# Four graph layers on one core: node batches started inside the edge sums, and window sums added into SBUF by VectorE

## The chip, the cores and the metric

The kernel runs on one core of one Trainium2 chip. The metric is the device time of that core in microseconds, the median of the runs of a kernel. The kernel before took 8477.11 us (median of 3 runs, 8463.03 to 8496.4). Its profile is one more execution, which took 6808.89 us; every duration taken from the profile belongs to that execution.

Names of engines: PE is TensorE, DVE is VectorE, ACT is ScalarE, POOL is GpSimd, SP is the engine that issues most DMAs.

## The reference

6,250 nodes with 128 features and 100,000 edges sorted by target node go through four layers. Each layer is added to its input and normalized by row.

```python
x = _layernorm(x + L0(x, edges))                 # two attention convolutions
x = _layernorm(x + L1(x, edges, edge_weight))    # weighted graph convolution
x = _layernorm(x + L2(x, node_vec, edges, ...))  # relational attention, 8 heads
x = _layernorm(x + L3(x, edges))                 # messages summed by target, then a gated unit

# L0, for each of its two convolutions (edges and self loops):
g = h @ W; e = leaky_relu(s[src] + d[dst]); m = segment_max(e, dst)
ex = exp(e - m[dst]); z = segment_sum(ex, dst)
out = segment_sum(g[src] * (ex / z[dst])[:, None], dst) + bias
# L1: out[dst] += (x @ W)[src] * dis[src] * w * dis[dst];   L3: agg[dst] += (h @ W_msg)[src]
# L2: softmax by target of q[dst] . k(message), times v(message); message from x[src] and the relation
```

The targets are drawn as 6250 times the square of a uniform number, so low node numbers have many more edges than high ones.

## The kernel before, in words

**Blocks and steps.** Nodes lie in NB = 49 blocks of 128. Edges are brought into K = 832 steps; a step holds at most 128 edges, all of one block of targets, and blocks come in rising order. `SRCT` holds the source node of each edge, `DLT` its place in the block, `OFF` the window offsets of the steps. The layout is made at the start (lines 134 to 289), where a flag (`unsorted`, lines 181 to 188) branches past a sort that this input doesn't need.

**Edge stages.** Five stages sum over all steps: `attention_edges` twice (lines 434 to 533), `sum_edges` for the convolution (line 681, weighted by the edge) and for the last layer (line 1010), and the value sum of layer 2 (lines 940 to 958). In the first four, each step begins with one gather of 128 rows from a table in HBM, an indirect DMA that POOL issues (`gather`, lines 132 to 134). A matrix of zeros and ones, `sel`, with the step's edges as rows and the 128 places of the block as columns, is then multiplied by the gathered rows on PE, which adds the edges up by target.

**The sums (`Windows`, lines 388 to 432).** M = 8 steps share a window of up to 9 blocks, laid out over three PSUM banks, with two such windows in rotation. For each window PE writes zeros into the three banks (line 412), adds eight step products at an offset that it holds in a register (line 415), and adds the old sum of the window's first block with an identity matmul out of SBUF (line 422; with a factor, line 426, at the first window of an attention chunk). ACT then copies the whole window, 1,224 columns, to the accumulator `ACC` in SBUF (line 431). So the next window's line 422 waits for ACT's copy.

**Attention chunks.** `attention_edges` goes in chunks of T = 64 steps: 64 gathers, small matmuls for the target's term (lines 467 and 470), then a chain of scans on DVE and transposes on PE that finds the maximum by target (lines 475 to 522), then the scaling on ACT (line 532) and the sums. In the first pass `row_selections` (lines 373 to 385) makes a bf16 matrix from a row that SP loads to all partitions (`dlrow`, line 381, two pieces per 16 steps, two buffers).

**Node stages.** Between two edge stages lies work by node, for 13 groups of up to 4 blocks (`GROUPS`): merging the sums, transposes, the next layer's matmuls, and the table in HBM that the next edge stage gathers from (lines 625 to 638, 642 to 648, 658 to 680, 683 to 693, 746 to 767, 961 to 977, 998 to 1009). All of it begins after the last edge sum. A whole-row normalization (`stats`, `inverse_root`, `normalize`, lines 322 to 343) first collects the statistics of all 49 blocks, then takes the root, then scales block by block on DVE. The last node stage (lines 1011 to 1046) writes the output in two DMAs.

**The score stage of layer 2 (lines 769 to 871).** It walks all steps in groups of 4: `rows_of` issues 4 gathers from `XAt`, 4 loads of query rows and 2 row loads; `messages` forms the message; `keys` transposes it, copies it out of PSUM on ACT and multiplies by the key and value weights; `scores` follows every 16 steps. In trip n it issues `rows_of(n+1)`, `messages(n)`, `keys(n-1)`. After it, lines 873 to 936 join the maxima of all steps, with no gather.

**What sets the order.** [...] A scheduler in the building layer places the instructions of a region by data dependence and source order, and may move an instruction past others within the region; it doesn't move anything across an `If`.

## Time and profile before

| | us |
|---|---|
| median of the runs | 8477.11 |
| the profiled execution | 6808.89 |
| its span, first to last instruction | 6807.1 |
| POOL busy | 4198.3 |
| PE busy | 4236.0 |
| ACT busy | 2223.4 |
| DVE busy | 1797.6 |
| gathers, four edge stages | 3,328 |
| gathers, score stage | 832 |

The page gives the busy time of each engine, the span in 40 slices, and the groups of equal instructions with the idle time before them. The timeline of one engine lists its instructions with start, length and, in brackets, the idle time before and what ended it. A table by stage gives the busy time of every engine in chosen stretches of the span; the stretches that the prediction shows begin and end at the first and the last gather of a stage. [...]

### The profile page before, as it was taken

How to read it: one execution, taken by the hardware profiler on the slowest of the kernel's cores; microseconds unless marked ns; L12 is line 12 of the kernel's file. 1: busy time of each engine (PE TensorE's matmuls, PEld its weight loads, DVE VectorE, ACT ScalarE, POOL GpSimd, SP SyncE). 2: the span in 40 equal slices, each digit the busy share in tenths (PEclk: the TensorE clock that was granted, in tenths of full speed). 3: DMA queues.
4: the chain of work that ended last, by engine and by line, in shares of the span. 5: the costliest groups of instructions: out<-in, count | busy, mean ns of one | idle time of the engine just before them, and what ended most of it. 6: DMA issues, size and time to landing. Idle time of an engine off the chain costs nothing. (4 is left out here: it accounts for less than half of the span.)

```text
span 6807.1 us, 75064 instructions
## 1 busy us (share of the span) xinstructions
PE 4236.0 (62%) x21755; PEld 2971.6 (44%) x21755; DVE 1797.6 (26%) x4328; ACT 2223.4 (33%) x5686; POOL 4198.3 (62%) x4384
## 2 busy tenths in 40 slices
PE   3355554434454546666656888888867756767676
PEld 2244433333343434444434556555545544444443
DVE  4122222300000040000017777777730030000005
ACT  1243333233333323444434444455412221111112
POOL 1777777277777627777753666666524426777771
PEclk9566666666556665555557989999968875555557
DMA  4455555344444333333336888899746634333331
GB/s 121 142 159 153 160 166 146 106 125 122 129 134 141 107 93 108 103 108 102 109 86 189 238 239 245 245 260 261 228 144 203 207 103 125 103 108 102 109 102 32
DMA packets 736418, 997.90 MB, mean 147 GB/s; under 512 B 151184, under 2 KB 593352, under 8 KB 702744
## 3 DMA queue, kind: packets, MB, share of 16 engines
q1 hardware_dynamic: 587410, 662.03, 30.3%
q0 software_dynamic: 146992, 331.03, 19.3%
q8 instruction: 197, 3.23, 0.2%
q14 instruction: 197, 1.61, 0.1%
q10 hardware_dynamic: 1622, 0.01, 0.0%
HBM read 824.55 MB, written 168.09 MB: 146 GB/s over the span
## 5 line engine op out<-in xcount | busy, mean ns | idle before, releaser
L415 PE MATMUL win<-g,sel 128*128 128x128 f32 (+2 forms) x6656 | 1710.9, 412 | 747.8 <-issue 250.8
L133 POOL DMA_INDIRECT g<-g,SRCT x1664 | 1578.6, 949 | 722.2 <-issue 492.9
L415 PEld LDWEIGHTS win<-g,sel 128*128 128x128 f32 x6656 | 1348.1, 288 | 1246.1 <-issue 457.3
L431 ACT COPY ACC<-win 128x1224 f32 x520 | 610.9, 1175 | 1992.4 <-PE win L422 1745.2
L133 POOL DMA_INDIRECT xa<-xat,SRCT x832 | 823.2, 989 | 538.8 <-issue 319.4
L133 POOL DMA_INDIRECT g<-yt,SRCT x832 | 785.0, 943 | 394.5 <-issue 388.1
L133 POOL DMA_INDIRECT g<-mt,SRCT x832 | 785.1, 944 | 355.0 <-issue 246.8
L412 PE MATMUL win<-zero 1*128 1x512 bf16 x1560 | 618.0, 495 | 32.4 <-ACT ACC L431 27.6
L549 ACT ACTIVATE g<-g,EWT 128x128 f32<-128x128 f32 x832 | 318.5, 399 | 608.8 <-DMA g<-yt,SRCT 607.3
L532 ACT ACTIVATE g<-g 128x128 f32<-128x128 f32 x1664 | 516.5, 390 | 0.0
L835 PE MATMUL pk<-Wkv,mT 128*128 128x256 f32 x1664 | 461.0, 409 | 32.3 <-ACT mT L828 22.7
L952 POOL TENSOR_TENSOR vx<-v,exh 128x512 f32<-128x512 f32 x208 | 217.7, 1062 | 424.4 <-PE win L415 268.2
L422 PE MATMUL win<-ACC,ident 128*128 x982 | 270.8, 371 | 157.9 <-ACT ACC L431 157.8
L415 PE MATMUL win<-vx,sel 128*128 128x136 f32 x1664 | 281.4, 337 | 124.2 <-issue 118.1
L835 PEld LDWEIGHTS pk<-Wkv,mT 128*128 128x128 f32 x1664 | 300.8, 199 | 95.4 <-ACT mT L828 53.8
L840 ACT COPY kv<-pk 128x512 f32<-128x512 f32 x416 | 242.2, 589 | 302.1 <-issue 187.9
L415 PEld LDWEIGHTS win<-vx,sel 128*128 128x128 f32 x1664 | 265.7, 242 | 155.7 <-issue 145.4
L477 DVE TENSOR_TENSOR de<-de,g 128x16 f32<-128x16 f32 x104 | 17.2, 184 | 1093.9 <-DMA g<-g,SRCT 1093.9
L422 PEld LDWEIGHTS win<-ACC,ident 128*128 128x128 f32 x982 | 221.6, 277 | 170.1 <-ACT ACC L431 170.1
L1029 DVE SCALAR_TENSOR_TENSOR n<-pn,bhh,gate 128x512 f32<-128x512 f32 (+1 forms) x13 | 9.4, 720 | 1053.5 <-ACT gate L1021 1053.0
L483 PE MATMUL pch<-ident,e 128*64 128x128 f32 x26 | 10.8, 416 | 443.6 <-DVE e L479 443.6
L814 ACT ACTIVATE z<-rp,TMT 128x128 f32<-128x128 f32 x832 | 238.2, 374 | 145.5 <-DVE msg L811 143.5
(329 smaller groups left out, 4878.0 us busy)
## 6 DMA issues: line engine op xcount, KB each, us to landing
sel<-seld SPq DMA_DIRECT2D x208, 1024.0 KB
qb<-qt SPq DMA_DIRECT2D x832, 102.0 KB
seld<-sel SPq DMA_DIRECT2D x52, 1024.0 KB
vt<-kv SPq DMA_DIRECT2D x208, 256.0 KB
v<-vt SPq DMA_DIRECT2D x208, 256.0 KB
g<-g,SRCT POOLq DMA_INDIRECT x1664
dlrow<-dlr SPq DMA_DIRECT2D x104, 256.0 KB
rseld<-rsel SPq DMA_DIRECT2D x52, 512.0 KB
```

Source lines behind the costliest of these rows:

```text
L133: nc.gpsimd.indirect_dma_start(out=dst_tile, out_offset=None, in_=tab, in_offset=bass.IndirectOffsetOnAxis(ap=idx, axis=0))
L412: nc.tensor.matmul(self.win[:, i, :], zero[:, 0:P], zero, start=True, stop=False, skip_group_check=True)
L415: nc.tensor.matmul(flat_[:, ds(self.at[q], n)], sel, rows, start=False, stop=False, skip_group_check=True)
L422: nc.tensor.matmul(self.win[:, 0, 0:n], ident, ACCF[:, ds(before, n)], start=False, stop=True, skip_group_check=True)
L431: nc.scalar.copy(ACCF[:, ds(self.to[w], (M + 1) * W)].rearrange("p (b w) -> p b w", b=SB), self.win[:, :, 0:SB * W])
L477: nc.vector.tensor_add(de[:, i * U:(i + 1) * U], de[:, i * U:(i + 1) * U], g[:, :, D])
L532: nc.scalar.activation(g[:, q, 0:D], g[:, q, 0:D], AF.Copy, scale=g[:, q, D:D + 1])
L549: nc.scalar.activation(g[:, q, :], g[:, q, :], AF.Copy, scale=EWT[:, k0 + q:k0 + q + 1])
L814: nc.scalar.activation(z[:, q, :], rp[:, q, D:], AF.Copy, scale=TMT[:, k0 + q:k0 + q + 1])
L835: nc.tensor.matmul(pk[:, q - q0, :], mT[:, q, :], Wkv, start=True, stop=True)
L840: nc.scalar.copy(kv[:, q0:q0 + 2, :], pk)
L952: nc.gpsimd.tensor_mul(vx[:, :, 0:D].rearrange("p q (h d) -> p q h d", h=HD), v.rearrange("p q (h d) -> p q h d", h=HD), exh[:, u0:u0 + B, ...
```

## The change

**Node batches ahead.** Each node stage between edge stages becomes a generator (`to_second`, `to_convolution`, `to_queries`, `to_messages`, `to_output`) for one group of 4 blocks, with a `yield` between its parts. While an edge stage runs, `Ahead.tick` is called after each window and advances one batch by one part; batch j starts at step EARLY[j]. Eleven of the 13 groups have such a place. A flag in a register, made from the layout at the start, says whether a block of these groups still had edges at its place; if so, all eleven are done again in an `If` after the stage. The last two groups (5 blocks) follow the `If`, part by part in turn.

**Windows.** A window now spans 3 steps (attention, values) or 4 (the two `sum_edges`) in one PSUM bank, with four banks in a ring. `ACC` is set to zero at the start of the stage; DVE adds the bank to `ACC` at an offset that DVE loads itself. The identity matmul and ACT's copy are gone; the factor of an attention chunk is applied to `ACC` by DVE.

```diff
-M = 8
-SB = 3
-T = 64
+WINDOWS = {3: W, 4: D}
+CHUNKS = [48] * 17 + [16]
+T = max(CHUNKS)
+EARLY = [236, 332, 408, 472, 528, 580, 628, 672, 712, 756, 792]
+NE = len(EARLY)
...
+        for j, k in enumerate(EARLY):
+            nc.vector.tensor_scalar(lates[:, j:j + 1], bkrow[0:1, k:k + 1], (j + 1) * B - 0.5, None, op0=OP.is_lt)
...
+    late = nc.values_load(lati, min_val=0, max_val=NE)
...
+    class Ahead:
+        def tick(self, k):
+            if k - self.last < 4 and k < K:
+                return
+            self.last = k
+            if self.on is None and self.j < NE and k >= EARLY[self.j]:
+                self.on = self.batch(*GROUPS[self.j])
+                self.j += 1
+            if self.on is not None and next(self.on, self) is self:
+                self.on = None
+        def finish(self, again=None):
+            while self.on is not None or self.j < NE:
+                self.tick(K)
+            with tc.If(late > 0):
+                if again is not None:
+                    nc.sync.dma_start(X[:, 0:NE * B, :], again)
+                for j in range(NE):
+                    for _ in self.batch(*GROUPS[j]):
+                        pass
+            rest = [self.batch(*g) for g in GROUPS[NE:]]
+            while rest:
+                rest = [r for r in rest if next(r, self) is not self]
...
+            for t0 in range(0, NB + MW, 14):
+                nc.vector.memset(ACC[:, t0:min(NB + MW, t0 + 14), :], 0.0)
...
+            bank = self.ring[:, k // m % self.banks, :]
+            if k % m == 0:
+                nc.tensor.matmul(bank[:, 0:m * w], zero[:, 0:P], zero[:, 0:m * w], start=True, stop=False,
+                                 skip_group_check=True)
+                self.fade = None
+            nc.tensor.matmul(bank[:, ds(self.at[k % U], n)], sel, rows, start=False, stop=False,
+                             skip_group_check=True)
...
+                if self.fade is not None:
+                    a0 = ACCF[:, ds(to, kept)]
+                    nc.vector.tensor_scalar(a0, a0, self.fade, None, op0=OP.mult)
+                a0 = ACCF[:, ds(to, m * W)].rearrange("p (b w) -> p b w", w=W)[:, :, 0:n]
+                nc.vector.tensor_add(a0, a0, bank[:, 0:m * w].rearrange("p (b w) -> p b w", w=w)[:, :, 0:n])
+                self.ahead.tick(k + 1)
```

**One batch, as an example.** The merge with the own rows is now done by PE with diagonal matrices, and the normalization is per batch (`norms` on DVE with a root by bit shift and three Newton steps, `normalized` on ACT):

```diff
+        def to_convolution(t0, g):
+            cc = merge_factors(node, SD[1], t0, g)
+            own = own_rows(node, Gt[1], t0, g)
+            yield
+            dg = diagonals(node, (cc[:, 0], cc[:, 1]), g, 2)
+            yield
+            px = batch_of(bank())
+            add_rows(px, g, bl1, t0)
+            for q in range(g):
+                nc.tensor.matmul(px[:, q, :], dg[:, q, 0, :], ACC[:, t0 + q, 0:D], start=False, stop=False,
+                                 skip_group_check=True)
+                nc.tensor.matmul(px[:, q, :], dg[:, q, 1, :], own[:, q, :], start=False, stop=q == g - 1,
+                                 skip_group_check=True)
+            r, m = norms(node, px, g)
+            yield
+            x = X[:, t0:t0 + g, :]
+            normalized(x, px, r, m, g)
+            nc.sync.dma_start(nodes(XS[0])[:, t0:t0 + g, :], x)
+            yield
+            xT = transposed(node, batch_of(bank("nb")), x, g, "hT")
+            yield
+            py = batch_of(bank())
+            for q in range(g):
+                nc.tensor.matmul(py[:, q, :], xT[:, q, :], W1l, start=True, stop=True)
+            y = node.tile([P, B, D], F32, name="own")
+            nc.vector.tensor_mul(y[:, :g], py[:, :g], DIS[:, t0:t0 + g, None].to_broadcast([P, g, D]))
+            nc.sync.dma_start(nodes(Yt)[:, t0:t0 + g, :], y[:, :g])
```

**Buffers.** The node work of layers 0 and 1 shares two single PSUM banks, `na` and `nb`, also for the very first node stage, where there were two buffers each for the transposes and the first product. Gather buffers of 16 steps go from 7 to 6 (attention), stay at 8 in the last `sum_edges` and go from 8 to 6 in the other. The row pieces of the first pass are halved and have one buffer:

```diff
-            for h in range(2):
-                n = U * P // 2
-                row = work.tile([P, n], BF16, name="dlrow")
+            for h in range(4):
+                n = U * P // 4
+                row = work.tile([P, n], BF16, name="dlrow", bufs=1)
```

**Score stage.** Gather buffers `xa` go from 4 to 8, query rows `qb` from 3 to 4, `kv` from 2 to 3, row selections of 4 steps to 4, and the transpose gets a trip of its own. The head's key-bias term of the queries comes from a matmul with a small weight matrix made at the start.

```diff
-                for n in range(-1, steps + 1):
+                for n in range(-1, steps + 2):
                     if n + 1 < steps:
-                        got[n + 1] = rows_of((n + 1))
+                        got[n + 1] = rows_of(n + 1)
                     if 0 <= n < steps:
                         msgs[n] = messages(n, got[n][0], got[n][3])
-                    if 0 <= n - 1:
-                        keys(n - 1, msgs.pop(n - 1), *got.pop(n - 1)[1:3])
+                    if 0 <= n - 1 < steps:
+                        turns[n - 1] = turned(msgs.pop(n - 1))
+                    if 0 <= n - 2:
+                        keys(n - 2, turns.pop(n - 2), *got.pop(n - 2)[1:3])
```

**Output.** `to_output` writes each batch to HBM as soon as it is normalized, in place of two DMAs at the end.

## The prediction, as put on record

> **What bounds the kernel now.** I read the 40 slices first, then the table by stage, then POOL's timeline inside a stage, then the groups. In the slices, POOL stands at seven tenths through most of the kernel, with dips:
>
> ```profile
> POOL 1777777277777627777753666666524426777771
> ```
>
> The table by stage cuts the span at the first and last gather of each stage. Rows in order: start, first attention pass, gap, second pass, gap, convolution sums, gap, score stage, gap, value sums, gap, message sums, end. Columns after the stretch: its length, busy time (instructions) of PE, its weight loads, DVE, ACT and POOL, the granted PE clock, the DMA share, GB/s.
>
> ```profile
> core 0: us, PE busy (x) PEld busy (x) DVE busy (x) ACT busy (x) POOL busy (x), PEclk, DMA share, GB/s
> 0.00:140.00 140.00, 49.80 (x236) 35.06 (x237) 59.56 (x122) 24.11 (x47) 8.76 (x16) 0.99 0.48 112
> 140.00:1185.80 1045.80, 519.14 (x3828) 398.94 (x3827) 217.73 (x432) 357.63 (x1017) 792.45 (x832) 0.61 0.53 155
> 1185.80:1304.40 118.60, 66.75 (x325) 53.89 (x326) 55.01 (x104) 44.81 (x110) 0.01 (x1) 0.66 0.28 83
> 1304.40:2354.20 1049.80, 470.29 (x2956) 362.02 (x2955) 60.68 (x265) 352.31 (x971) 786.13 (x832) 0.60 0.44 129
> 2354.20:2495.40 141.20, 59.20 (x343) 48.29 (x343) 82.70 (x276) 42.10 (x102) 0.00 (x0) 0.67 0.24 69
> 2495.40:3533.60 1038.20, 656.69 (x2168) 438.05 (x2168) 0.00 (x0) 423.50 (x932) 784.92 (x832) 0.54 0.35 105
> 3533.60:3659.80 126.20, 41.07 (x157) 31.61 (x157) 106.34 (x298) 38.74 (x70) 0.04 (x1) 0.66 0.40 124
> 3659.80:4895.60 1235.80, 1067.92 (x6596) 719.93 (x6597) 947.59 (x2085) 600.12 (x1892) 823.15 (x832) 0.94 0.87 249
> 4895.60:5015.20 119.60, 64.28 (x308) 41.58 (x307) 77.75 (x218) 18.82 (x52) 0.07 (x1) 0.61 0.26 67
> 5015.20:5537.80 522.60, 377.39 (x2135) 308.51 (x2135) 32.17 (x55) 143.34 (x303) 217.74 (x208) 0.82 0.65 207
> 5537.80:5639.50 101.70, 42.55 (x229) 31.02 (x228) 69.00 (x226) 20.35 (x35) 0.00 (x0) 0.71 0.13 39
> 5639.50:6677.90 1038.40, 731.54 (x2169) 456.61 (x2170) 0.00 (x0) 121.36 (x103) 785.06 (x832) 0.53 0.35 105
> 6677.90:6807.10 129.20, 89.43 (x311) 46.09 (x311) 89.09 (x248) 36.23 (x56) 0.00 (x0) 0.83 0.10 26
> ```
>
> Four stages issue 832 gathers each and last 1038 to 1050 us, whatever else is in them. POOL's timeline tells why; each line has start, length, and in brackets the idle time before and what ended it:
>
> ```profile
> 1305.70 0.94 POOL L133 DMA_INDIRECT g<-g,SRCT  x1 [0.31 <-issue]
> ```
>
> A gather holds POOL for 0.94 us and 0.31 lie between two: 1.248 us each, and 832 of them are 1038 us. So these stages are POOL's own rate of issue, and no sum, copy or PE work in them is on the path. On the path besides: the start, the six stretches without gathers (118.6 + 141.2 + 126.2 + 119.6 + 101.7 + 129.2 = 736.5 us), and the score and value stages, which have other limits.
>
> [...] 944 ns a gather with DVE at 0% (convolution), 989 ns with DVE at 77% (score stage). [...]
>
> **Part 1: the window sums.** Out of the groups (busy and mean ns, then idle time before and its releaser):
>
> ```profile
> L431 ACT COPY ACC<-win 128x1224 f32 x520 | 610.9, 1175 | 1992.4 <-PE win L422 1745.2
> L412 PE MATMUL win<-zero 1*128 1x512 bf16 x1560 | 618.0, 495 | 32.4 <-ACT ACC L431 27.6
> L422 PE MATMUL win<-ACC,ident 128*128 x982 | 270.8, 371 | 157.9 <-ACT ACC L431 157.8
> ```
>
> Removed: ACT 611 us, PE 618 + 291 (with 20 us of L426 and L429). Added: one zero matmul per window: 278 in each of two attention passes and the value sums, 208 in each of two plain sums, 1,250 in all, at most 0.4 us each, so under 500 us on PE. DVE adds 384 to 512 columns from PSUM; 256 columns cost 413 ns and 512 cost 682, so by interpolation 0.56 us (attention, 384 of 396 columns), 0.57 (values) and 0.68 (plain sums): 556 x 0.557 + 278 x 0.573 + 416 x 0.682 = 753 us. Each add also loads an offset. All of it but the values' share lies in POOL-bound stages where DVE was 0 to 21% busy: cost nothing as long as DVE keeps up. If that cover goes, up to 150 to 280 us of DVE work per stage show. Behind a waiting add stand DVE's scans and the node work; PE waits for a bank only when four windows are out, i.e. 12 to 16 steps, 15 to 20 us of gathers.
>
> What could show is the gather itself: 45 ns more at 77% DVE, so with DVE at 30 to 50% I take 11 ns each, 3,328 x 0.0135 with chunk joints = **+45 us**. Bounds: 0, and +250 us if the attention chunks, now 48 steps (60 us of gathers), don't keep up. In the first pass the selection row has one buffer instead of two: 12 loads per chunk at about 2.8 us (a load took 3 us from issue to landing) are 34 us and 23 us of DVE work against 60; it fits, narrowly. SP issues those loads and the new batch stores; POOL gets only branches.
>
> **Part 2: node batches move under the sums.** Of 13 batches 11 leave each gap; the flag is 0 for these sources and targets (the blocks at the eleven places are 4, 8, ... 36, 41, 44, none below what it needs), so the redo is a branch. An existing branch on a loaded flag has a price on DVE:
>
> ```profile
> 30.23 1.09 DVE L190 TENSOR_TENSOR RF<-RF,DP 128x896 f32<-128x896 f32 x1 [1.38 <-DVEq L186]
> ```
>
> 1.4 us each, five in all, inside the figures below. What stays in a gap: the last sums behind the last gather, the branch, two batches in turn, table store and first gather.
>
> - Gap 1: the last gather ends at 1185.8 and the last sum near 1245 for 64 steps, so some 59 us; the last chunk is now 16 steps, so about 20, plus 5 blocks of merge and matmuls in series (about 28) and the first gather 3: 51. **-68.**
> - Gap 2: as gap 1 with one more transpose and two matmuls: 55. **-86.** The 12.6 us of scaling after the statistics is gone too.
> - Gap 3: 4 us of sums, about 30 of batches, 8 to load weights and fetch rows: 42. **-84.**
> - Gap 4 joins maxima after the scores, unchanged but for a setting of `ACC` to zero: 122. **+2.**
> - Gap 5: 36. **-66.** End: 2 batches of six parts (about 40) and an output DMA of about 9 us: 52. **-77.**
> - Start: the first node stage isn't moved; it gets single banks where it had two. It took 2.8 us a batch (13 batches from 99.5 to 136 us); one bank means the copy out stands in series, 5.6: 13 x 2.8 = **+38** (bounds +10 to +60).
>
> Moved DVE, ACT, PE and SP work per stage is 50 to 80 us each, under 1038 us of gathers: nothing, unless a batch's wait holds DVE past four windows.
>
> **Part 3: score and value stages.** In the score stage all engines are near one another. Per 4 steps: POOL 4 x 1.29 = 5.15 us, PE 5.0, DVE 4.5; the stage takes 1235.8 / 208 = 5.94. POOL waits for DVE:
>
> ```profile
> L133 POOL DMA_INDIRECT xa<-xat,SRCT x832 | 823.2, 989 | 538.8 <-issue 319.4 <-DVE z L815 165.6 <-DVE SC L858 19.3
> ```
>
> The 165.6 + 19.3 us are waits for buffers. The change splits `keys` into two trips, so that PE's transposes don't wait for ACT's copy (L835 waits 22.7 us on it), and PE has three trips in flight. Floor: POOL, 832 x 1.25 = 1040. I take 5.43 per 4 steps, about two thirds of the way from 5.94 down to POOL's 5.15: 208 x 5.43 = 1130, **-106**; bounds 0 and -196. With DMA already at 87% a faster stage moves the same bytes in less time (0.87 x 1236 / 1130 = 95%), a reason not to take the floor.
>
> The value stage is PE-bound: 20.1 us per 32 steps. It loses about 94 us of PE work (zeros and identities) and gains 278 zeros and eleven batches x 6.7 = 74 us: **+2**, bounds -60 to +60.
>
> **Sum**, in the profiled execution: 6808.9 + 38 - 68 - 86 - 84 + 2 - 66 - 77 + 45 - 106 + 2 = **6409**. The runs' median is 8477.11 / 6808.89 = 1.245 times it. I carry the ratio, as I have no sign that one stage alone takes the difference: 6409 x 1.245 = **7980**. If savings carried over in us, 8477 - 400 = 8077.
>
> **Rivals.**
>
> - *A, as summed*: 7980, own range 7870 to 8100. Chance 0.52.
> - *B, gaps close, the rest gives back*: score stage unchanged because DMA at 87% is its limit, edge stages +100 (late chunk buffers), values +25. 6808.9 - 341 + 125 = 6593, so 8208. For it: the DMA share. Against: POOL's 185 us of waits on buffers. Chance 0.20.
> - *C, all parts at the good end*: start +10, edges +20, score -146, values -35: 6808.9 - 369 - 161 = 6279, so 7817. Chance 0.14.
> - *D, slower*: DVE's new work holds POOL's issue in the edge stages. Without the +45 the sum is -445, so it decides from 445 / 3328 = 0.134 us a gather; at 0.2 it is 6364 + 666 = 7030, so 8752. For it: [...] 989 is above 944. Against: that is 0.045 at 77% DVE. Chance 0.10.
> - *E, nothing moves*: the scheduler leaves the batches behind the sums, or a redo costs what the batches save; within 0.5%, about 8477. The order on each engine has them between window adds. Chance 0.04.
>
> 0.5% is about what a measurement of this kernel can tell from no change. Faster by more: A, B, C, 0.86; within: E, 0.04; slower: D, 0.10. The range 7760 to 8250 holds A, B and most of C, and leaves D, E and the tails out.
>
> **What would show it.** Right: in the stage table the gaps 1, 2, 3, 5 and the end at 36 to 55 us, edge stages at 1040 to 1065 with gathers near 955 ns, the start at 178, the score stage near 1130, L431 and L422 gone. Wrong: gathers over 1.07 us (D); POOL waiting for a sum or a scaling in the attention passes (B); ten or more batches in a gap (E); a ratio of runs to profile other than 1.245, which would move the total with every stage right.

## The result, and the profile after

The changed kernel takes 9019.74 us (median of 4 runs, 8995.6 to 9054.06) against 8477.39 us for the kernel before on the same chip: 1.0639 times as long, interval 1.0611 to 1.0666. The forecast was 7980.

The runs of this study fall into two kinds, told apart by the time of the kernel before on the same chip: 8344 to 8497 us in the one (kind P), 6807 to 6813 in the other (kind Q). No chip showed both, but only five chips were told apart (three P, two Q) and only one was used in two sittings, so that the kind belongs to the chip is likely and not shown. The result above is of kind P; the profile of before that the prediction was worked from (6808.89) matches kind Q. So both kernels were profiled in both kinds, the kernel before as `c_before` on P, the changed one as `after_2` on Q. On kind Q the changed kernel takes 7140.21 us against 6812.95: 1.048 [1.0462, 1.0497]. It is slower there as well, so the kind does not explain the sign.

The slices of after on kind P, and its groups (busy and mean ns of one, then the idle time before them and its releaser):

```profile
POOL 0544444525555552665554355555512223656562
...
L141 POOL DMA_INDIRECT g<-g,SRCT x1664 | 1583.1, 951 | 1848.4 <-issue 617.2
L498 PE MATMUL ring<-zero 1*128 1x408 bf16 (+1 forms) x1250 | 624.5, 500 | 2608.6 <-DVE ACC L511 1743.8
L511 DVE TENSOR_TENSOR ACC<-ACC,ring 128x512 f32 (+3 forms) x1250 | 758.5, 607 | 4165.3 <-remote 2081.6
```

ACT's copy L431 and the identity L422 are gone. The 1,250 adds (L511) cost what was forecast, 758.5 us on DVE against 753. The zeros (L498) take 624.5 us on PE, 0.50 us each, where at most 0.4 each and under 500 in all were forecast. A gather still takes 951 ns. The new entry is the idle time of PE ahead of L498: 1743.8 us of waiting for DVE's add. The seven tenths of POOL have become four and five.

The table by stage of `after_2` (kind Q) is the one to lay beside the prediction's. Same rows: start, first pass, gap, second pass, gap, convolution sums, gap, score, gap, values, gap, messages, end.

```profile
core 0: us, PE busy (x) PEld busy (x) DVE busy (x) ACT busy (x) POOL busy (x), PEclk, DMA share, GB/s
0.00:219.88 219.88, 99.12 (x330) 69.54 (x331) 64.03 (x165) 25.25 (x46) 8.82 (x16) 0.71 0.37 85
219.88:1469.45 1249.57, 649.34 (x3811) 477.88 (x3811) 416.95 (x1020) 263.07 (x953) 794.20 (x832) 0.53 0.47 129
1469.45:1597.26 127.81, 82.83 (x378) 62.21 (x377) 59.45 (x178) 26.41 (x87) 0.00 (x1) 0.53 0.31 93
1597.26:2665.57 1068.31, 637.09 (x3059) 451.73 (x3060) 268.64 (x954) 264.13 (x946) 791.51 (x832) 0.55 0.45 130
2665.57:2778.34 112.77, 74.27 (x295) 51.49 (x295) 49.35 (x193) 24.86 (x83) 0.00 (x1) 0.64 0.23 72
2778.34:3823.85 1045.51, 618.89 (x2156) 432.40 (x2155) 191.45 (x442) 351.97 (x911) 792.13 (x832) 0.54 0.37 113
3823.85:3928.11 104.26, 75.51 (x306) 58.02 (x305) 35.32 (x121) 15.69 (x33) 0.00 (x1) 0.61 0.22 70
3928.11:5081.47 1153.36, 1014.87 (x6452) 669.82 (x6452) 927.30 (x2054) 598.27 (x1854) 818.83 (x832) 0.99 0.93 263
5081.47:5222.71 141.24, 81.45 (x456) 51.42 (x454) 97.35 (x261) 31.57 (x90) 0.00 (x0) 0.70 0.36 93
5222.71:5992.88 770.17, 587.90 (x2050) 391.13 (x2051) 241.35 (x605) 71.85 (x265) 221.13 (x208) 0.59 0.48 149
5992.88:6061.21 68.33, 43.04 (x147) 25.64 (x147) 29.09 (x97) 6.54 (x15) 0.01 (x2) 0.65 0.22 72
6061.21:7105.19 1043.98, 696.64 (x2173) 429.14 (x2173) 215.17 (x504) 47.36 (x89) 790.61 (x832) 0.59 0.35 108
7105.19:7144.90 39.71, 17.96 (x53) 9.74 (x53) 11.16 (x49) 6.04 (x13) 0.00 (x0) 0.63 0.10 21
```

Three places hold the loss: the value stage went from 522.6 to 770.2 us, the first pass from 1045.8 to 1249.6, the start from 140.0 to 219.9. Second pass, convolution and messages stayed near POOL's pace (1068.3, 1045.5 and 1044.0 us against 832 x 1.248 = 1038); score stage and end got shorter about as forecast; gap 1 grew by 9 us, and gaps 2, 3 and 5 shrank far less than forecast.

### The profile page after: what moved, and what is told of

The parts are those of the page before. It is cut to its first block, busy times and chain, and to the rows that moved or that the text cites. A ratio compares the mean times of both kernels' runs of the same rounds, so it can differ in the third digit from the quotient of the medians.

```text
span 8993.8 us, 78446 instructions
## 1 busy us (share of the span) xinstructions
PE 4848.7 (54%) x21656; PEld 3312.3 (37%) x21656; DVE 2610.6 (29%) x6638; ACT 1705.2 (19%) x5383; POOL 4212.0 (47%) x4384
## 5 line engine op out<-in xcount | busy, mean ns | idle before, releaser
L501 PEld LDWEIGHTS ring<-g,sel 128*128 128x128 f32 x6656 | 1436.8, 312 | 3027.1 <-issue 2772.0
L498 PE MATMUL ring<-zero 1*128 1x408 bf16 (+1 forms) x1250 | 624.5, 500 | 2608.6 <-DVE ACC L511 1743.8
L511 DVE TENSOR_TENSOR ACC<-ACC,ring 128x512 f32 (+3 forms) x1250 | 758.5, 607 | 4165.3 <-remote 2081.6
L501 PE MATMUL ring<-g,sel 128*128 128x128 f32 (+2 forms) x6656 | 1736.6, 429 | 182.1 <-issue 145.0
L607 ACT ACTIVATE g<-g 128x128 f32<-128x128 f32 x1664 | 502.6, 387 | 19.6 <-issue 15.9
L501 PEld LDWEIGHTS ring<-vx,sel 128*128 128x128 f32 x1664 | 347.3, 293 | 287.5 <-issue 257.1
L501 PE MATMUL ring<-vx,sel 128*128 128x136 f32 x1664 | 435.9, 422 | 28.5 <-POOL vx L1119 12.3
L961 PE MATMUL pq<-qb,rsel 128*128 128x136 bf16 x2496 | 250.9, 245 | 26.3 <-DMA xa<-xat,SRCT 16.4
L929 PE MATMUL rp<-RT,oty 128*128 128x256 bf16 x832 | 254.4, 306 | 2.5 <-issue 0.5
L498 PEld LDWEIGHTS <-zero 1*128 1x128 bf16 x1250 | 126.2, 101 | 345.8 <-issue 325.7
L930 PE MATMUL rp<-RT,oty 64*128 64x256 bf16 x832 | 250.8, 301 | 0.0
L961 PEld LDWEIGHTS <-rsel 128*128 128x128 bf16 x2496 | 212.7, 111 | 85.5 <-issue 50.3
```

The lines of the kernel that those rows point to most:

```text
L498: nc.tensor.matmul(bank[:, 0:m * w], zero[:, 0:P], zero[:, 0:m * w], start=True, stop=False, skip_group_check=True)
L501: nc.tensor.matmul(bank[:, ds(self.at[k % U], n)], sel, rows, start=False, stop=False, skip_group_check=True)
L511: nc.vector.tensor_add(a0, a0, bank[:, 0:m * w].rearrange("p (b w) -> p b w", w=w)[:, :, 0:n])
L607: nc.scalar.activation(g[:, q, 0:D], g[:, q, 0:D], AF.Copy, scale=g[:, q, D:D + 1])
L929: nc.tensor.matmul(rp[:, q, :], oty[:, o:o + P], RT2, start=True, stop=False)
L930: nc.tensor.matmul(rp[:, q, :], oty[0:REL, o:o + P], RT3, start=False, stop=True)
```

## Experiments

My theory when I began: the ring of four banks is written as one PSUM tile, the scheduler keeps dependences by tile, so a zero matmul waits for the add of the window just before. Rivals: the sums' adds and the moved batches slow the gathers (D of the prediction); the batches hold the sums up; the slower PE of kind P accounts for the result. The runs, with before on the same chip:

| run | us | before | ratio [95%] |
|---|---|---|---|
| c_before | 8477.37 | 8497.42 | single run |
| ring4 | 8625.11 | 8497.42 | 1.0143 [1.0124, 1.0162] |
| w_only | 9719.78 | 8497.42 | 1.1426 [1.1402, 1.145] |
| ring4_row | 8534.09 | 8483.45 | 1.0062 [1.0039, 1.0085] |
| ring4_fill | 9310.61 | 8483.45 | 1.0984 [1.096, 1.1008] |
| b_fill | 8587.37 | 8483.45 | 1.0138 [1.0114, 1.0161] |
| fixA | 8204.75 | 8343.9 | 0.9833 [0.9813, 0.9853] |
| b_score | 8341.18 | 8343.9 | 0.9994 [0.9981, 1.0008] |
| b_half | 8233.45 | 8343.9 | single run |
| fixA_late | 7203.33 | 6807.96 | 1.0582 [1.0564, 1.06] |
| b_none | 6777.67 | 6807.96 | single run |
| after_2 | 7140.21 | 6812.95 | 1.048 [1.0462, 1.0497] |
| fixA_2 | 6456.31 | 6812.95 | 0.9479 [0.946, 0.9499] |
| ring4_2 | 6676.13 | 6806.72 | 0.9806 [0.979, 0.9822] |
| fixB | 6448.12 | 6806.72 | 0.9474 [0.9458, 0.949] |

`after_2` is the changed kernel as it is, on kind Q:

> The changed kernel as it is, once more, beside the kernel before on the same chip; what counts is on which kind of chip it lands. Two kinds have shown: before takes 8340 to 8500 us on the one (PE has slow stretches), 6808 us on the other (it has none, the profile shown of before is of that kind). Theory A (the loss of 6.4% comes from the slow stretches, in which the one PSUM tile and the single buffers lie on the path): on a chip of the second kind edge stages at 1040 to 1100 us, time 6400 to 6800 us, faster than before; on the first kind 1.06 again. Theory B (one tile and single buffers cost the same everywhere): slower than before by 4 to 8% on either kind.

Its 1.048 is what Theory B expected.

### The ring as four tiles: ring4, ring4_2

```diff
-        ring = psum.tile([P, 4, BANK], F32, name="ring")
+        ring = [psum.tile([P, BANK], F32, name=f"ring{i}") for i in range(4)]
...
-            bank = self.ring[:, k // m % self.banks, :]
+            bank = self.ring[k // m % self.banks]
```

Same banks, same instructions; only the unit by which dependences are kept differs.

> The changed kernel with four PSUM tiles of one bank instead of one tile of four banks. In the changed kernel's trace each zero matmul waits for the add of the window just before it, so PE and DVE take turns (3.36 us per window of 4 steps, 2.74 per window of 3). Theory A (these turns are what stretches the edge stages from 1040 to 1290-1680 us): with four tiles the zero matmul runs three windows ahead, the five sum stages lose 100 to 250 us each, and the time falls from 9020 to 8000-8500 us. Theory B (the turns are covered, and what stretches the stages is the node work and scans that stand in the queues of ACT and DVE): within 1.5% of 9020 us.

> The changed kernel with four PSUM tiles of one bank and nothing else, for a chip of the second kind (before at 6808 us; after_2 took 7140 there, fixA_2 6456). Theory A (one tile is the larger part of the 684 us between those two): value stage from 770 to 460 us, gaps 1 to 3 shorter by 20 to 60 us each, first attention pass still above 1200 (its row has one buffer), time 6600 to 6800. Theory B (the single row buffer is the larger part): time 6850 to 7050. On a chip of the first kind: 1.014 of before again.

First what there was to remove. The timeline of PE and DVE in the value stage of `after_2`:

```profile
5501.08 0.58 DVE L511 TENSOR_TENSOR ACC<-ACC,ring 128x408 f32 x1 [2.24 <-PE ring L501]
5501.71 0.49 PE L498 MATMUL ring<-zero 1*128 1x408 bf16 x1 [0.67 <-DVE ACC L511]
...
5502.13 1.73 PE L501 MATMUL ring<-vx,sel 128*128 128x136 f32 x6
...
5503.90 0.58 DVE L511 TENSOR_TENSOR ACC<-ACC,ring 128x408 f32 x1 [2.24 <-PE ring L501]
...
5504.53 0.49 PE L498 MATMUL ring<-zero 1*128 1x408 bf16 x1 [0.67 <-DVE ACC L511]
```

PE and DVE take turns: add, 0.67 us, zero, products, add. One turn is 5503.90 - 5501.08 = 2.82 us, and 278 windows at 770.17 / 278 = 2.77 us are the stage. PE's and DVE's work no longer lie beside each other although three banks are empty. With four tiles the waits of PE (us in total, times, longest) change from this in `after_2`

```profile
PE ring L498 <- DVE ACC L511: 1081.5, 932, 11.0
```

to this in `ring4_2`,

```profile
PE ring L498 <- DVE ACC L511: 257.0, 57, 15.3
```

and its value stage (table by stage, `ring4_2`) from 770.17 to

```profile
5099.31:5553.18 453.87, 394.33 (x2124) 288.96 (x2124) 267.80 (x637) 61.90 (x264) 217.66 (x208) 0.89 0.82 253
```

453.87 us, with PE's granted clock up from 0.59 to 0.89. That is 68.7 us less than before's 522.6. In all the edit is worth 7145 - 6683.5 = 461 us of span on kind Q: values -316, gaps 1, 2, 3 and 5 -149, first pass -58, second pass +62. It alone turns the sign on kind Q (0.9806 against 1.048). On kind P 1.0143 is left of 1.0639; 8625 us lies between the ranges of the two theories for `ring4`. There the value stage loses as much as on kind Q (770.1 to 459.0 us), but the first pass gets longer by 193 us (1678.1 to 1870.9): POOL's waits in it for PE's products (L501), which free the gather buffers, rise from 271 to 651 us. So the theory holds for the value stage and the gaps. It does not hold for the first pass, which is still 1191.7 us on kind Q.

### The row pieces: ring4_row

```diff
-            for h in range(4):
-                n = U * P // 4
-                row = work.tile([P, n], BF16, name="dlrow", bufs=1)
+            for h in range(8):
+                n = U * P // 8
+                row = work.tile([P, n], BF16, name="dlrow", bufs=3)
```

> Four PSUM tiles as in ring4, and the row for the selections loaded in 8 pieces of 256 into three buffers instead of 4 pieces of 512 into one. In ring4 the first attention pass is 1871 us, with 52 us without a gather in every 48 steps, and DVE waits for a piece 3.3 us at a time between the steps of its chain. Theory A (the one buffer strings the loads along DVE's chain): pieces come about twice as fast, the first pass falls to 1450-1650 us, the time to 8200-8420. Theory B (the chunks of 48 steps are too short for the chain, whoever feeds it): the first pass stays above 1800 us and the time within 1% of 8625.

The first pass went from 1870.9 us in `ring4` to 1785.0, on kind P; both theories missed it. The two ran on different chips, where the first pass of the kernel before took 1453 and 1442 us, so some 75 of the 86 us are the edit's. What the single buffer does is plain in DVE's timeline in `ring4`:

```profile
1035.15 0.35 DVE L466 TENSOR_SCALAR rsel<-dlrow,relid 128x512 bf16<-128x512 bf16 x1 [4.16 <-DMA dlrow<-dlr]
1035.42 0.30 DVE L570 TENSOR_TENSOR_SCAN car<-scf,car,pch 1x48 f32<-1x48 f32 x1
...
1038.54 0.35 DVE L466 TENSOR_SCALAR rsel<-dlrow,relid 128x512 bf16<-128x512 bf16 x1 [2.64 <-DMA dlrow<-dlr]
1042.07 0.35 DVE L466 TENSOR_SCALAR rsel<-dlrow,relid 128x512 bf16<-128x512 bf16 x1 [3.18 <-DMA dlrow<-dlr]
```

Each piece can only be loaded when DVE has used the one before, so each L466 (0.35 us of work) waits 2.6 to 4.2 us for its load, and the chain of the chunk that holds the gather buffers (L570 and what follows) stands in the same queue behind these waits. Two pieces of 1024 columns in two buffers (`fixA`, below, kind P, a third chip) leave the pass at 1572.5.

### Batches where they were: w_only, fixA_late

In `tick`: `if k < K: return`, so no batch begins before the last step. `w_only` is the changed kernel with it, `fixA_late` is `fixA` with it.

> The changed kernel, but no batch starts before the last step of its stage: all 13 batches follow the sums, as before; windows, chunks and score stage are the changed ones. Theory A (turns of PE and DVE over the one PSUM tile): the edge stages stay at 1250 us and more, gaps grow by 60 to 100 us each, the time is 9300 to 9500 us. Theory B (node batches block ACT and DVE): edge stages fall back to 1040-1060 us, gaps are 110 to 150 us, the time is 8300 to 8600 us.

> fixA with no batch before the last step of its stage, as in w_only: with the single buffers gone, what is the early start of the batches worth? Theory A (the batches ahead are what fixA gains by): gaps 2, 3, 5, 1 and the end are 80 to 240 us longer each, edge stages 0 to 60 us shorter, time 0.05 to 0.09 above fixA's ratio of 0.983, so 1.03 to 1.07. Theory B (moved into the edge stages the batches cost there what they save in the gaps): within 0.01 of 0.983.

If batches under the sums were what hurts, these would be quicker. They are the slowest of their families: `w_only` 9719.78 on kind P, above the 9500 that Theory A allowed; `fixA_late` 7203.33 against 6456.31 for `fixA_2`, both on kind Q, though not on one chip (before 6808 and 6813). The stages without gathers show it: gaps 2, 3, 5 and the end are 284, 260, 234 and 245 us in `fixA_late`, 99, 36, 46 and 39 in `fixA_2`. Moving the batches works, and is worth 747 us of these batches. It has to be: unhidden they are dearer than the old ones (`before` had 141, 126, 102 and 129). On kind Q the edge stages pay next to nothing for them (none differs by more than 6 us between the two runs). On kind P they seem to pay in part: in `w_only` the convolution takes 1193.2 us and the second pass 1384.3, where `after`, with batches in them, has 1306.1 and 1443.3 (not run side by side); the messages take 19 us more and the first pass is the same within 5 us. The value stage pays 460.8 - 348.6 = 112 us for the batches in it, where 74 were forecast.

### All single buffers doubled: fixA, fixA_2, fixB

Beside `ring4`: the start takes turns over three pairs of banks; row pieces of 1024 in two buffers (room from `own`, `fw`, `tot` made single); the two halves of `pks` and `pqs` in the score stage become tiles of their own.

```diff
+        for i, (t0, g) in enumerate(GROUPS):
+            def turn(name="na", i=i):
+                return ring[i % 3 * 2 + (name == "nb")] if i % 3 < 2 else bank(name)
...
+            for h in range(2):
+                n = U * P // 2
+                row = work.tile([P, n], BF16, name="dlrow")
...
+                        pk = psum.tile([P, 2, 2 * D], F32, name="pk", bufs=2)
+                        pq_ = psum.tile([P, 2, W], F32, name="pq", bufs=2)
```

> ring4 with three more undone parts, each in a stage of its own: the first node stage turns over three pairs of PSUM banks instead of one pair; the row for the selections comes in 2 pieces of 1024 into two buffers as in the kernel before (room for it from single buffers of four small tiles); the score stage has two PSUM tiles each for keys and queries instead of one with two halves. Theory A (what is left of the change's loss is single buffers): start from 219 to 150-165 us, first attention pass from 1871 to 1500-1650, score stage from 1560 to 1450-1530, time 8080 to 8350 us, under the 8480 of before. Theory B (the length of the chunk, and PE's own pace, set the first pass): start as above, first pass above 1750, time 8420 to 8560 us.

> fixA (four PSUM tiles, paired buffers) once more, for the kind of chip. On the second kind, from the trace of the same kernel with late batches (edge stages 1049, 1162, 1038, 1038, score 1106, values 349) and the gaps of fixA (163, 99, 105, 100, 145, 46, 114): 6350 to 6600 us, 0.93 to 0.97 of before. On the first kind 0.983 again.

`fixB` gives `fw` and `tot` their second buffer back and takes four row pieces in three buffers, to find out what lengthened the second pass.

> fixA with the two scan tiles of the attention chain double again and the row in 4 pieces of 512 into three buffers. fixA_2 has a second attention pass of 1160 us, 92 more than the changed kernel. Theory A (making the scan tiles single cost that): second pass 1055 to 1080 us, first pass 1050 to 1070, time 6340 to 6390 on a chip of the second kind (0.93 to 0.94 of before). Theory B (the four PSUM tiles changed the order of DVE's queue there): second pass stays near 1160, and ring4_2 shows it too. On a chip of the first kind 0.97 to 0.985.

On kind P `fixA` is the first version that beats before (0.9833); on kind Q `fixA_2` and `fixB` take 5.2 and 5.3% off. Against `ring4_2`, `fixA_2` is shorter by 60 us in the start (219.9 to 160.3), 138 in the first pass (1191.7 to 1053.5) and 35 in the score stage (1151.9 to 1116.6). DVE's waits for the row loads fall as the theory has it: in `ring4_2`

```profile
DVE rsel L466 <- DMA dlrow<-dlr: 534.9, 169, 5.4
```

and in `fixB`

```profile
DVE rsel L466 <- DMA dlrow<-dlr: 153.0, 58, 5.9
```

Its table by stage, first pass, second pass and values:

```profile
157.55:1202.76 1045.21, 477.26 (x3953) 375.49 (x3954) 433.99 (x1077) 273.03 (x992) 791.86 (x832) 0.65 0.55 160
...
1265.73:2427.68 1161.95, 538.60 (x3077) 405.87 (x3077) 270.27 (x955) 262.64 (x935) 789.48 (x832) 0.60 0.41 121
...
4856.33:5315.13 458.80, 393.30 (x2124) 289.19 (x2124) 272.98 (x634) 61.84 (x264) 218.91 (x208) 0.89 0.82 250
```

The first pass is back at POOL's pace, 1045.21, with DVE at 434 us. In it POOL waits 3 us for ACT's reads of the gather buffers (L602, L604, L607), where in `after_2` it waited 188. The second pass is not: 1161.95, where `after_2` had 1068.31. Double scan tiles did not help (1160.3 with single ones), so these are not its cause; `ring4_2`, which never had them single, has 1130.2. About 62 us of the 94 came with the four tiles alone. DVE's and POOL's timelines of `fixB` show what holds the pass:

```profile
1799.49 0.18 DVE L554 TENSOR_TENSOR de<-de,g 128x16 f32<-128x16 f32 x1 [18.38 <-DMA g<-g,SRCT]
1799.79 0.21 DVE L556 SCALAR_TENSOR_TENSOR e<-de 128x48 f32<-128x48 f32 x1
1800.10 0.31 DVE L552 TENSOR_REDUCE de<-pdn 128x48 f32<-128x144 f32 x1
1800.32 0.15 DVE L597 SCALAR_TENSOR_TENSOR fac<-pch,OH 128x1 f32<-128x1 f32 x1
...
1806.37 0.94 POOL L141 DMA_INDIRECT g<-g,SRCT  x1 [8.46 <-PE ring L501]
```

On DVE the factor of one chunk (L597), without which its sums can't be added, stands behind the first steps of the next chunk (L554), which wait 18.38 us for that chunk's last gathers. So the sums start late, their gather buffers come free late, and POOL issues nothing for 8.46 us. In this pass POOL waits 123.5 us for L501 in `fixB` and 27.1 in `after_2`; that is 96 us more, and the pass is 94 longer. In `after_2` the factor is ahead of the next chunk's steps:

```profile
2034.94 0.15 DVE L597 SCALAR_TENSOR_TENSOR fac<-pch,OH 128x1 f32<-128x1 f32 x1
...
2044.00 0.19 DVE L554 TENSOR_TENSOR de<-de,g 128x16 f32<-128x16 f32 x1 [6.81 <-DMA g<-g,SRCT]
```

The order is the scheduler's. A version that forces the other order was not tried, so this cause is read from the timelines and not shown by a run.

### The score stage's order alone: b_score

Before, with the changed score section and its two PSUM tiles split (`rsel` 4 deep).

> The kernel before with the changed order of the score stage alone (keys a trip later, more buffers for the gathered rows), with two PSUM tiles each for keys and queries. Theory A (the order alone gave the 90 to 120 us by which the score stage got shorter, 1649 to 1530-1560): score stage 1500 to 1560 us, time 8340 to 8400. Theory B (the stage got shorter since something else moved out of it): within 0.5% of before.

0.9994 [0.9981, 1.0008] on kind P: no difference. The stage is 26 us shorter than in `b_half`, whose score stage is the old one (1538.5 against 1564.4), and the gap after it 24 longer. So on that chip the section was worth nothing in the total: what the stage lost, the gap got. In whole changed kernels the stage is 82 to 125 us shorter on kind Q. On kind P the unchanged stage itself took 1649.0, 1617.9 and 1564.4 us on three chips; beside these, each on its chip, it is shorter by 89 in `ring4`, 88 in `ring4_row` and 47 in `fixA`. What part of this the section earns was not told apart.

### Kind P itself: c_before, b_half, b_none, b_fill, ring4_fill

> The kernel before, unchanged, with a profile of the same kind of execution as its timed runs. Theory A (the profile shown of before is of an execution on other terms than its timed runs, and the changed kernel's is not): this profile has a span near 8477 us rather than 6807, and the extra 1670 us lie in the stretches with gathers, which no longer last 832 x 1.248 = 1038 us. Theory B (both profiles are on the same terms, and the timed runs of before carry something outside the span): span near 6807, gather stages at 1038 to 1050 us.

`c_before` is the kernel before, unchanged. Its table by stage on kind P, convolution and value sums:

```profile
3203.76:4405.64 1201.88, 460.47 (x1868) 334.86 (x1868) 0.00 (x0) 312.85 (x802) 786.85 (x832) 0.58 0.28 87
...
6373.06:6890.75 517.69, 372.39 (x2134) 304.53 (x2135) 32.15 (x55) 143.40 (x303) 217.74 (x208) 0.83 0.65 209
```

Values: 517.7 against 522.6 on kind Q, no difference; convolution 1201.9 against 1038.2. So 1.245 is not one factor for all stages. All of the excess lies in the five stages with gathers (408, 261, 413, 164, 250 us) and some gaps (28 + 13 + 71 + 66). POOL's gathers are not slower (787 us for 832). The convolution in PE's timeline, `c_before`:

```profile
3246.61 2.29 PE L415 MATMUL win<-g,sel 128*128 128x128 f32 x9
3250.20 0.37 PE L415 MATMUL win<-g,sel 128*128 128x128 f32 x1 [1.30 <-issue]
3253.00 0.37 PE L415 MATMUL win<-g,sel 128*128 128x128 f32 x1 [2.43 <-issue]
3255.11 0.37 PE L415 MATMUL win<-g,sel 128*128 128x128 f32 x1 [1.74 <-issue]
3257.90 0.37 PE L415 MATMUL win<-g,sel 128*128 128x128 f32 x1 [2.42 <-issue]
```

The passes of a step's product come 2.80, 2.11 and 2.79 us apart and wait for nothing that the profile shows. These gaps are four, three and four times 0.70 us. In `before` six such passes take 1.89 us:

```profile
2709.50 1.89 PE L415 MATMUL win<-g,sel 128*128 128x128 f32 x6
```

To count this beat, take PE's completions from the semaphore events of the trace, and of them the stretches of at least four in a row whose distances all lie within 0.03 us of a multiple of 0.70. They fill 16 us of `before` and none of `after_2`, `ring4_2`, `fixA_2` and `fixB`. On kind P they fill 462 us of `c_before`, 712 of `after`, 1051 of `ring4` and 1947 of `fixA`; a limit of 0.05 us gives 807 for `c_before` and still 16 for `before`. So the beat tells the kinds apart. It does not measure the time lost: `fixA` has the most of it and is the quickest changed version on kind P, and the score stage of `c_before`, 413 us longer, has 6 us of it. Nor does it go with the granted clock: that is 0.58 in the convolution of `c_before` and 0.54 in that of `before`, and in the score stage, with 6 us of the beat, 0.81 and 0.94.

What the longer stages wait for is on POOL. In the first pass of `c_before`:

```profile
POOL g L133 <- PE win L415: 369.2, 28, 41.1
```

In `before` this wait is 2.4 us. In the second pass it is 219.3 against 12.7, in the messages 224.4 against 5.5, and in the convolution 56.0 against 2.7 with 115.2 us more whose releaser the profile doesn't tell. So on kind P PE finishes the products late, the gather buffers come free late, and these stages are no longer at POOL's pace. In the score stage POOL waits for DVE (L815) 514.9 us against 165.6. The other runs asked what brings the beat on:

> The kernel before; in its two plain edge sums the matmul of every second step is left out, so that half of the edges aren't added there (gathers, scalings, zero and identity matmuls stay). Theory A (slow stretches of PE come with PE's load, and PE's pace sets these stages): convolution and message stages fall from 1202 and 1288 us to 1040-1080, the time by 300 to 400 us. Theory B (they come where PE is mostly idle): these stages stay above 1180 us.

> The kernel before; in its two plain edge sums PE keeps one step matmul of eight, one zero matmul of three and the identity matmul per window (ACT copies the first bank three times), so that seven eighths of the edges aren't added there; gathers and scalings stay. Theory A (PE's pace is what stretches these stages beyond POOL's 832 x 1.25 us): both stages fall to 1040-1060 us. Theory B (something else does, gathers landing late or ACT): they stay above 1150.

> The kernel before with one idle-filling matmul of 512 columns into a spare bank after every step of its two plain edge sums, nothing else changed. Theory A (slow stretches come where PE is mostly idle): convolution and message stages fall from 1202 and 1288 us to 1040-1120 us, the time to 8100-8250. Theory B: the stages lengthen, the time is 8500 to 8900 us.

> As ring4_row, and in the two plain edge sums (convolution, messages) PE gets two idle-filling matmuls of 512 columns into a bank of its own after every step; windows there have three banks instead of four. In the timed executions PE has stretches in which its completions lie 0.70 us or multiples of it apart, 370 to 590 us in each of these stages by the changed kernel's and ring4's traces. Theory A (these stretches come where PE is mostly idle; in the dense value stage of ring4 there is none): convolution and message stages fall from 1260 to 1040-1120 us and the time by 250 to 400 us against ring4_row. Theory B (they come with PE's load, or are independent of it): the added 0.4 to 0.85 us per step lengthen these stages by 100 us or more each.

`b_half` leaves every second step's product out of the two plain sums: these stages lose 24 and 77 us of 1203 and 1279 (`b_score`, on the same chip), and the beat fills 723 and 576 us of them, where it was 430 and 290. So half the products gone did not take the beat away; of the messages' excess over 1038 us a third went. `b_none` leaves out seven of eight products and two of three zeros there; it ran on kind Q, where its 1038.5 us are POOL's pace anyway, and tells nothing on the beat. More PE work in small pieces (`b_fill`) made the time 1.0138 [1.0114, 1.0161]. With 1,024 columns of zeros after each step (`ring4_fill`) the completions were on the beat for less time (330 to 127 us in the convolution, 475 to 151 in the messages, against `ring4_row` on the same chip), but these stages got 270 and 208 us longer. Its convolution in the table by stage:

```profile
3632.79:5161.02 1528.23, 1385.83 (x3487) 576.21 (x3485) 188.26 (x438) 354.91 (x911) 785.79 (x832) 0.51 0.25 76
```

PE is 91% busy and is granted 0.51. What sets a stretch off stays open.

## Why the prediction was wrong, step by step

Forecast and measured changes against the same profile of before, in us of span on kind Q, and those of `fixB`:

| | forecast | after_2 | fixB |
|---|---|---|---|
| start | +38 | +80 | +18 |
| gap 1 | -68 | +9 | -56 |
| gap 2 | -86 | -28 | -43 |
| gap 3 | -84 | -22 | -89 |
| gap 4 | +2 | +22 | +18 |
| gap 5 | -66 | -33 | -55 |
| end | -77 | -89 | -90 |
| four edge stages | +45 | +235 | +121 |
| score stage | -106 | -82 | -125 |
| value stage | +2 | +248 | -64 |
| sum (before rounding) | -400 | +338 | -365 |

- **The step that failed: "PE waits for a bank only when four windows are out".** I counted banks and took them for buffers. The code has one tile with four slices, so a zero waits for the add of one window ago. This is shown by `ring4_2`: -461 us on kind Q, of which 316 are in the value stage, the one stage of sums where PE and not POOL sets the pace. In the edge stages a turn of 3.4 us per four steps (3.36 in the convolution of `after`) lies under 4 x 1.25 = 5 us of gathers, and on kind Q the cover that the prediction named held: 1045.5 us for the convolution and 1044.0 for the messages in `after_2`. For the value stage I had put the new adds down as work beside PE, where they were in series with it: +248 us instead of +2. The gaps contain such turns as well (-30, -30, -67 and -22 us in gaps 1, 2, 3 and 5 with four tiles).
- **The +2 of the value stage did not follow from its own terms either.** -94 and +74 leave 22 us for 278 zeros, which at the 0.4 us allowed to each are 111. With four tiles the windows alone took 174 us off (348.6 in `fixA_late` against 522.6) and the batches gave 112 back, so both terms were too small, in opposite directions.
- **"34 us and 23 us of DVE work against 60; it fits, narrowly"** failed by the queue, not the sum. A wait for a load took 2.7 us in the mean of `after_2` (419.8 us in 155 waits), near the 2.8 I took; but each wait stands ahead of the chunk's chain on DVE: in the timeline of `ring4` above L570 comes right behind an L466 that had waited 4.16 us. The prediction has scans standing behind a waiting add and did not ask the same of a waiting load. First pass +204 us; -58 with the ring, -146 more with the row's three buffers and the rest of `fixB`, which were not told apart on kind Q.
- **Start, a mis-sized term.** In `after_2` most batches follow one another by 8.7 us (ACT's copies), not 5.6: with one bank each for `na` and `nb` a batch's transposes, copy, product and tables are all in series, not just the one copy. +80 instead of +38 (13 x 2.8 is 36); pairs of banks bring +18.
- **Gap 4**, +22 against +2, and it is +18 in `fixB` too: whatever causes it is not the single tiles. It comes with the score section: `b_score`, which changes that alone, has +24. By estimate it is a moved border: with eight gather buffers in place of four the gathers can end four trips earlier, and four trips of 1153 / 208 = 5.5 us are 22 us of scores behind the last gather. As much of the score stage's gain is then no gain. No run shows this apart.
- **What was right.** The gathers themselves hardly slow: 950 to 953 ns in `after_2` against 943 to 949 before, with DVE at 18 to 33% in the edge stages. That is 4 to 9 ns more by gathered table, where I had put 11 by estimate and rival D 200; D's mechanism is refuted though its sign came true. What the window adds and what the batches' other operations have of these few ns was not measured apart. The end came out at 39.7 us (forecast 52), the score stage at 1153 (1130). With the single buffers undone, gaps 3 and 5, the end and the score stage are within 19 us of the forecast. `fixB`'s span, 6442, is 0.5% above the 6409 that I had summed, but this is luck: errors that cancel, values 66 us better than forecast, score and start 39 better; the second pass 112 us longer than before where some 11 were allowed, gap 2 43 worse than forecast.
- **Carrying the ratio 1.245** was the second fault. It assumed the extra time spread evenly, "as I have no sign that one stage alone takes the difference". `c_before` shows none of it in the value stage, the start and gap 5. On kind P the changed kernel loses 114 us more in the second pass than on kind Q and 97 more in the convolution, the two stages that the change alone should have left at POOL's pace. `w_only` has no such loss in the convolution (1193 us, before 1202 on the same chip), which points to the moved batches there, though `after` and `w_only` were not run side by side; in the second pass `w_only` is 59 us shorter than `after`. The ratio was still the smaller fault: of the 1040 us by which 7980 fell short, (7140 - 6409) x 1.245 = 910 are the sum's, and some 130 come from the changed kernel's own ratio between the kinds, 9019.74 / 7140.21 = 1.263.

The rivals had banks only as a thing that may run out. None had "the ring has four banks and one owner", although the slice `self.ring[:, k // m % self.banks, :]` in the diff says so. The prediction's own test, "POOL waiting for a sum", came nearest.

## What to carry to other kernels

Under this scheduler a ring was as deep as the number of tiles that it could tell apart, not as the number of banks (the value stage took 770.17 us with one tile and 453.87 with four, on the same four banks): look for the wait of the first writer on the last reader, and ask of which turn that reader is. Price a single buffer by what stands behind its wait in the same queue, not by the sum of its loads: with DVE's waits for the row down from 534.9 us (`ring4_2`) to 153.0 (`fixB`, with what else it changes), the first pass went from 1191.7 to 1045.2. Before a ratio between runs and a profile is carried over, compare them stage by stage on the chip where the time is to be told.

## What the runs showed of the hardware that I had not expected

- On chips of kind P, PE's results come for long stretches (462 us of `c_before` in all, 16 of `before`) at distances of 0.70 us or multiples of it, and in the convolution of `c_before` the passes of a product follow 2.1 to 2.8 us apart, where six take 1.89 us in `before`, 0.3 each. The granted clock of that stage is no lower: 0.58 against 0.54. No run shows what causes the beat.
- In the convolution of `ring4_fill`, on kind P, PE was busy for 91% of 1528 us, more than half of it with products of a one-row zero operand (701.5 and 112.4 us, L625 and L498), and was granted 0.51. In the value stage of `ring4_2`, on kind Q, it was busy for 87% of 453.87 us and was granted 0.89, and in that of `ring4_fill` itself for 86% of 456.40 us and granted 0.89. So busy time of the first mix did not bring the higher clock; which part of it made the difference was not tried.
- A kernel's time on kind P is not its time on kind Q times a factor: the changed kernel's ratio to before is 1.0639 on P and 1.048 on Q, `ring4`'s 1.0143 and 0.9806, on opposite sides of no change.
